# A gated cross-attention layer with a mixture of experts: the dispatch of tokens rewritten

## The chip, the core and the metric

The kernel runs on one core of one Trainium2 chip. The core has TensorE (matmuls; PE in the profile, its weight loads PEld), VectorE (DVE), ScalarE (ACT), GpSimd (POOL) and SyncE (SP), each with a queue of instructions that it works off in order. SyncE, ScalarE and GpSimd also start transfers (DMAs), which run on 16 engines that all of them share. The metric is the time on the device in microseconds (us), lower being better; the median of several runs is compared.

## The reference

The layer has two halves. In the first, 4096 tokens `x` of 512 numbers, normalised, attend to 3202 context rows, and four feature groups of each token go through the weights `W_qv`; the result, times tanh of a gate, is added to `x`. The second half is a mixture of eight experts:

```python
xf = layernorm(x)
gates = softmax(xf @ w_router + b_router)
topv, topi = top_k(gates, 2)                     # two experts for each token
cap = int(1.25 * n / e)                          # 640 places for each expert
onehot = one_hot(topi.reshape(-1), e)
pos = cumsum(onehot, axis=0)[arange, e_flat] - 1 # the token's place with its expert
keep = pos < cap
buf = zeros(e, cap, d).at[e_flat, posc].add(where(keep, xf[tok], 0))
h = gelu(einsum('ecd,edf->ecf', buf, w1) + b1)
out = einsum('ecf,efd->ecd', h, w2) + b2
# each kept token gets its experts' rows back, weighted by its gates over their sum
x = x + tanh(g_ffn) * y
```

What matters here: the places are handed out in the order of the tokens, so they need a running count per expert; and no expert can start before every token has been put in its place.

## The kernel before, in words

The tokens lie in tiles of 128 (`NT` = 32 tiles). The kernel has three stages.

**Attention** (to about 1532 us of the profile) works in eight groups of four tiles. It leaves behind, in DRAM, the transposed normalised tokens (`qT_d`) and a partial result for each tile (`r_d`). It also fills the experts' buffer `buf_d` with empty rows.

**Dispatch** (1532 to about 1700 us, lines 835 to 1054) takes the tiles in steps: seven steps of four and two of two (`STEPS`, line 877). `tile_mm` (line 882) loads a tile's share of `qT_d` and its `r` (three buffers), does eight matmuls into a PSUM tile `x1p` (line 895), lets VectorE add `r` to give the new token row `x1` (line 899), which ScalarE's queue stores to `out` (line 902). The logits of the router come from the same PSUM tile (lines 906 and 910). VectorE takes mean and variance of `x1` (lines 912 and 913).

`norms` (line 916) is called once for a step. GpSimd makes the scale 1/sqrt(variance + eps) for its tiles (lines 919 and 920, one addition and one power); VectorE scales the logits (922, 923); ScalarE writes the normalised row into `xn` (line 928).

`route` (line 932) chooses the two experts: maximum, exponentials (952), a one-hot mask for each choice (970 to 973), the sum `mask` (977), and the running counts `base` (984). `slots` (line 985) is called later: TensorE turns `mask` and `base` into positions in PSUM (987 and 988, `pos`); VectorE picks each choice's position and gate (994 to 997), tests it against `CAP`, divides the gates by their sum, writes them beside the row, and makes the row number `sidx` (1016 to 1022).

`dispatch` (line 1027) sends every tile twice: GpSimd starts an indirect DMA (line 1030) that scatters its 128 rows, 516 numbers each, to the rows `sidx` of `buf_d`; a row number past the end is dropped. There are 64 such scatters.

The order is that of the loop at its end: tiles of step g, `norms` of g, then `slots` and the scatters of step g - 2, then `route` of g - 1. A scheduler keeps this order on each queue where the instructions depend on each other, and may move others. So the scatters of a step stand on GpSimd's queue between the scales of two steps, and the positions of a step stand on TensorE's queue after the four tiles of a later step.

**Experts** (from about 1700 us). `expert_in` loads five blocks of 128 rows from `buf_d` (line 1128, three buffers `xb`), for expert 0 with a wait on all scatters; TensorE transposes them (line 111). Rows for the next expert are loaded during the present one. The weights come in halves: `load_half(e, h)` (line 827) loads 2 MB of `w1` (line 829) and 2 MB of `w2` (line 831) into one of two buffers each. Halves (0, 0) and (0, 1) are loaded in the dispatch, behind the loads of `qT_d` number 3 and 6 (line 887).

Of the kernel before, what the change touches and what calls it, by code (L numbers as in the profile page):

```python
# [14 lines left out]
P = 128  # L15
# [5 lines left out]
def gated_layer(ctx, tc, x, x_t, ctxt, ctxt_t, g_xattn, g_ffn, w_sim, w_sim1, b_sim, W_qv, W_qv_t, b_qv, b_qv_c, w_router, b_router, w1, b1, w2, b2, out):  # L21
# [814 lines left out]
    with ExitStack() as s2:  # L836
# [34 lines left out]

        scatters = []
        xg = {}
        prev_base = None


        STEPS = [list(range(t, t + G)) for t in range(0, NT - G, G)]
        STEPS += [list(range(t, t + G // 2)) for t in range(NT - G, NT, G // 2)]
        step_of = {t: k for k, ts_ in enumerate(STEPS) for t in ts_}
        qTs = {}  # L880

        def tile_mm(t, mv, lg):
            g, i = divmod(t, 4)
            if g not in qTs:
                qTs[g] = sb.tile([P, DC, TG], F32, name=f"q2T{g}", tag="q2T")
                ld = nc.sync.dma_start(qTs[g], qT_d[g])
                if g in (3, 6):
                    with tc.issue_after(ld.ins):
                        load_half(0, g // 6)
            r = sb.tile([P, 2, BW], F32, name=f"r2_{t}", tag="r2")  # L890
            nc.sync.dma_start(r, r_d[t])
            ps = ps_mm.tile([P, 2, 512], F32, name=f"x1p{t}", tag="mm")
            for j in range(2):
                for c in range(DC):
                    nc.tensor.matmul(  # L895
                        ps[:, j, :B1], qTs[g][:, c, i * P : (i + 1) * P], W1[:, c, j, :], start=(c == 0), stop=(c == DC - 1)
                    )
            x1 = sb.tile([P, D], F32, name=f"x1_{t}", tag="x1", bufs=G + 2)
            nc.vector.scalar_tensor_tensor(
                x1.rearrange("p (j d) -> p j d", j=2), ps[:, :, :256], tgx, r[:, :, :256], ALU.mult, ALU.add  # L900
            )
            nc.scalar.dma_start(out[t * P : (t + 1) * P, :], x1)

            k = t - STEPS[step_of[t]][0]
            l_ = lg[:, k, :]
            nc.vector.scalar_tensor_tensor(
# [3 lines left out]
            nc.vector.scalar_tensor_tensor(l_, ps[:, 1, 256:B1], sd[:, t : t + 1], l_, ALU.mult, ALU.add)  # L910
            st = sm.tile([P, 6], F32, name=f"st{t}", tag="st")
            nc.vector.bn_stats(st, x1)
            nc.vector.bn_aggr(mv[:, k, :], st)
            return x1

        def norms(k, x1s, mv, lg):
            n = len(x1s)
            rstd = sm.tile([P, G], F32, name=f"rstd{k}", tag="rstd")[:, :n]
            nc.gpsimd.tensor_scalar(rstd, mv[:, :n, 1], EPS, None, ALU.add)
            nc.gpsimd.tensor_tensor(rstd, rstd, neghalf.to_broadcast([P, n]), ALU.pow)  # L920
            l_ = lg[:, :n, :]
            nc.vector.tensor_tensor(l_, l_, rstd.unsqueeze(2).to_broadcast([P, n, E]), ALU.mult)
            nc.vector.tensor_tensor(l_, l_, br.unsqueeze(1).to_broadcast([P, n, E]), ALU.add)
            nb = sm.tile([P, G], F32, name=f"nb{k}", tag="nb")[:, :n]
            nc.vector.scalar_tensor_tensor(nb, mv[:, :n, 0], -1.0, rstd, ALU.mult, ALU.mult)
            xg[k] = sb.tile([P, G, R], F32, name=f"xn{k}", tag="xn", bufs=6)
            for i, x1 in enumerate(x1s):
                nc.scalar.activation(
                    xg[k][:, i, :D], x1, AF.Identity, scale=rstd[:, i : i + 1], bias=nb[:, i : i + 1]
                )  # L930

        def route(g, lg, prev):

            t0, n = STEPS[g][0], len(STEPS[g])

            def T(name, shape, dt=F32):
                a = sm.tile([G if k == "n" else G + 1 if k == "n+1" else k for k in shape], dt, name=f"{name}{g}", tag=name, bufs=3)
                return a[tuple(slice(0, n) if k == "n" else slice(0, n + 1) if k == "n+1" else slice(None) for k in shape)]

            def wide(a):  # L940
                return a.unsqueeze(2).to_broadcast([P, n, E])

            tt, ts, red = nc.vector.tensor_tensor, nc.vector.tensor_scalar, nc.vector.tensor_reduce
            revw = rev.unsqueeze(1).to_broadcast([P, n, E])
            mx = T("mx", [P, "n"])
            red(mx, lg, AX.X, ALU.max)
            d = T("d", [P, "n", E])
            tt(d, lg, wide(mx), ALU.subtract)

            ts(d, d, EXP_FLOOR, None, ALU.max)  # L950
            gate = T("gate", [P, "n", E])
            nc.scalar.activation(gate, d, AF.Exp)
            gs = T("gs", [P, "n"])
            red(gs, gate, AX.X, ALU.add)
            gi = T("gi", [P, "n"])
            nc.vector.reciprocal(gi, gs)
            tt(gate, gate, wide(gi), ALU.mult)


            oh = [T("oh0", [P, "n", E]), T("oh1", [P, "n", E])]  # L960
            rv = T("rv", [P, 2, "n"])
            eq = T("eq", [P, "n", E])
            left = T("left", [P, "n", E])
            for k in range(2):
                if k:
                    nc.vector.scalar_tensor_tensor(left, oh[0], -1000.0, d, ALU.mult, ALU.add)
                    red(mx, left, AX.X, ALU.max)
                    tt(eq, left, wide(mx), ALU.is_equal)
                else:
                    ts(eq, d, 0.0, None, ALU.is_equal)  # L970
                tt(eq, eq, revw, ALU.mult)
                red(rv[:, k, :], eq, AX.X, ALU.max)
                tt(oh[k], eq, wide(rv[:, k, :]), ALU.is_equal)


            mask = T("mask", [P, "n", E])
            tt(mask, oh[0], oh[1], ALU.add)
            base = T("base", [P, "n+1", E])
            if prev is None:
                nc.vector.memset(base[:, 0, :], 0.0)  # L980
            else:
                nc.vector.tensor_copy(base[:, 0, :], prev)
            for i in range(n):
                tt(base[:, i + 1, :], base[:, i, :], mask[:, i, :], ALU.add)
            def slots():
                ps = ps_po.tile([P, G, E], F32, name=f"pos{g}", tag="pos")[:, :n, :]
                nc.tensor.matmul(ps, upper, mask, start=True, stop=False)
                nc.tensor.matmul(ps, ones, base[:, :n, :], start=False, stop=True)

                pos = T("pos", [P, 2, "n"])  # L990
                gv = T("gv", [P, 2, "n"])
                tmp = T("tmp", [P, "n", E])
                for k in range(2):
                    tt(tmp, ps, oh[k], ALU.mult)
                    red(pos[:, k, :], tmp, AX.X, ALU.add)
                    tt(tmp, gate, oh[k], ALU.mult)
                    red(gv[:, k, :], tmp, AX.X, ALU.add)
                keep = T("keep", [P, 2, "n"])
                ts(keep, pos, float(CAP), None, ALU.is_lt)
                tt(gv, gv, keep, ALU.mult)  # L1000


                wsum = T("wsum", [P, "n"])
                tt(wsum, gv[:, 0, :], gv[:, 1, :], ALU.add)
                ts(wsum, wsum, 1e-6, None, ALU.max)
                nc.vector.reciprocal(wsum, wsum)
                ts(wsum, wsum, tgf, None, ALU.mult)  # L1007
                tt(
                    xg[g][:, :n, D : D + 2].rearrange("p g k -> p k g"),
                    gv, wsum.unsqueeze(1).to_broadcast([P, 2, n]), ALU.mult,  # L1010
                )
                nc.vector.tensor_copy(xg[g][:, :n, D + 2], tok[:, t0 : t0 + n])


                slot = T("slot", [P, 2, "n"])
                ts(slot, rv, -float(CAP), float(E * CAP), ALU.mult, ALU.add)
                tt(slot, slot, pos, ALU.add)
                ts(slot, slot, past, None, ALU.subtract)
                tt(slot, slot, keep, ALU.mult)
                sidx = T("sidx", [P, 2, "n"], I32)  # L1020
                ts(sidx, slot, past, None, ALU.add)
                nc.vector.tensor_copy(xg[g][:, :n, D + 3], sidx[:, 0, :])
                return sidx

            return base[:, n, :], slots

        def dispatch(g, sidx):
            for i in range(len(STEPS[g])):
                for k in range(2):
                    sc = nc.gpsimd.indirect_dma_start(  # L1030
                        out=buf_d[:, :],
                        out_offset=bass.IndirectOffsetOnAxis(ap=sidx[:, k, i : i + 1], axis=0),
                        in_=xg[g][:, i, :],
                        in_offset=None,
# [10 lines left out]
        for g in range(len(STEPS) + 1):  # L1045
# [4 lines left out]
            if half_routed is not None:  # L1050
                dispatch(g - 2, half_routed())
# [281 lines left out]
```

## Time and profile before

| What | Value |
|---|---|
| Median of 3 runs | 2716.5 us (2714.0 to 2717.52) |
| Profiled execution: its own time | 2714.11 us |
| Profiled execution: span, first to last instruction | 2712.3 us |
| TensorE busy in the span | 2642.9 us (97%) |
| VectorE busy | 1689.3 us (62%) |
| ScalarE busy | 419.8 us (15%) |
| GpSimd busy | 233.2 us (9%) |
| Mean granted TensorE clock | 0.984 of full speed |
| Dispatch: first and last matmul of a tile start | 1532.6 and 1657.8 us |
| Dispatch: first and last scatter start | 1583.6 and 1696.3 us |
| Experts: first transposition on TensorE | 1701.5 us |

The span is the time between the first and the last instruction of the one execution that the profiler recorded; the execution's own time lies 1.8 us above it. Times within the trace are counted from the span's start. A group of instructions is named by its line, engine, operation and tiles (written, then read). An engine's idle time is put down to what released it: `<-DVE mask L977` means that VectorE's instruction of line 977 came last of what was waited for; `issue` is time in which the profile shows nothing waited for. A matmul's end is modelled, so a busy TensorE is not a TensorE at its peak; the granted clock says how fast it was allowed to run.

### The profile page before, as it was taken

To read this page: it belongs to the slowest core of one execution; us is meant where nothing else is said; L and a number is where in the kernel's file an instruction comes from. 1 tells how busy PE (TensorE), PEld (TensorE's weight loads), DVE (VectorE), ACT (ScalarE), POOL (GpSimd) and SP (SyncE) were. 2 spreads that over 40 slices of the span, in tenths; PEclk is the share of its full clock that TensorE was granted. 3 is DMA by queue.
4 is the path that set the end of the run, shared out by engine and by line. 5 is a ranking of instruction groups with operands and counts; after the bars stand their busy time and mean duration, and the time that the engine had idled before them with its cause. 6 is when DMAs were issued, how large, how long until landed. Compare 5 with 4: busy or idle time off the path is not lost. (4 is left out here: it accounts for less than half of the span.)

```text
span 2712.3 us, 29984 instructions
## 1 busy us (share of the span) xinstructions
PE 2642.9 (97%) x11384; PEld 2130.5 (79%) x11384; DVE 1689.3 (62%) x3412; ACT 419.8 (15%) x673; POOL 233.2 (9%) x289
## 2 busy tenths in 40 slices
PE   8999999999999999999999994899999999999999
PEld 7648888888888888888888883677777777777776
DVE  7855755946837658459366576565747475655654
ACT  1200200201202102002011011111111111111111
POOL 0110000000001000000000036101001010101010
PEclk9898999999999999999999997899999999999999
DMA  7984765646746657467445794222323132322210
GB/s 260 270 296 174 190 208 155 226 159 175 229 154 173 230 154 227 155 181 234 147 145 187 241 362 142 90 86 94 112 105 118 68 124 86 132 82 105 82 59 20
DMA packets 184051, 436.65 MB, mean 161 GB/s; under 512 B 18616, under 2 KB 85165, under 8 KB 181858
## 3 DMA queue, kind: packets, MB, share of 16 engines
q1 hardware_dynamic: 157538, 357.48, 40.8%
q0 software_dynamic: 16624, 47.37, 5.3%
q10 hardware_dynamic: 9744, 29.87, 3.0%
q8 instruction: 90, 1.47, 0.2%
q14 instruction: 55, 0.45, 0.1%
HBM read 356.22 MB, written 85.60 MB: 163 GB/s over the span
## 5 line engine op out<-in xcount | busy, mean ns | idle before, releaser
L453 PE MATMUL pas<-Qp,kt 128*128 128x256 f32 (+1 forms) x728 | 175.5, 383 | 0.0
L1095 PE MATMUL pah<-bT,w 128*128 128x320 f32 x512 | 161.0, 437 | 0.8 <-DVE bT L1136 0.8
L570 PE MATMUL pbv<-E,vt 128*128 128x256 f32 (+1 forms) x728 | 159.5, 379 | 0.0
L570 PEld LDWEIGHTS pbv<-E,vt 128*128 128x128 f32 (+1 forms) x728 | 138.2, 190 | 18.9
L453 PEld LDWEIGHTS pas<-Qp,kt 128*128 128x128 f32 (+1 forms) x728 | 136.0, 188 | 21.4
L511 ACT ACTIVATE E<-E 128x1024 f32<-128x1024 f32 (+1 forms) x112 | 111.4, 996 | 156.5 <-DVE E L510 154.1
L510 DVE TENSOR_TENSOR E<-E,mb 128x1024 f32<-128x1024 f32 (+1 forms) x112 | 125.2, 1142 | 12.4 <-ACT mb L495 12.4
L1095 PEld LDWEIGHTS pah<-bT,w 128*128 128x128 f32 x512 | 98.0, 192 | 39.9 <-DVE bT L1136 1.2
L895 PE MATMUL x1p<-W,q2T 128*128 128x264 f32 x512 | 118.0, 391 | 3.3 <-DVE wsum L1007 1.6
L1095 PE MATMUL pao<-w,h 128*128 128x256 f32 x512 | 121.0, 379 | 0.0
L1270 POOL DMA_INDIRECT out<-acc,ti x40 | 42.8, 1070 | 859.4 <-DVE acc L1269 859.4
L895 PEld LDWEIGHTS x1p<-W,q2T 128*128 128x128 f32 x512 | 97.7, 192 | 21.2 <-PE x1p L895 3.6
L1247 PE MATMUL op<-w,h 128*128 128x512 f32 x256 | 113.7, 592 | 0.0
L471 DVE TENSOR_TENSOR M<-M,E 128x1024 f32<-128x1024 f32 (+1 forms) x96 | 109.0, 1136 | 6.7 <-ACT p1s L410 0.5
L1095 PEld LDWEIGHTS pao<-w,h 128*128 128x128 f32 x512 | 96.7, 190 | 16.7 <-issue 4.3
L410 ACT COPY p1s<-pas 128x512 f32<-128x512 f32 (+1 forms) x56 | 31.1, 554 | 499.0 <-issue 256.6
L426 DVE TENSOR_TENSOR E<-p4s,u3s 128x512 f32<-128x512 f32 (+1 forms) x56 | 36.5, 652 | 109.8 <-PE p4s L453 109.8
L522 DVE TENSOR_TENSOR SM<-SM,E 128x1024 f32<-128x1024 f32 (+1 forms) x80 | 89.1, 1114 | 0.0
L1247 PEld LDWEIGHTS op<-w,h 128*128 128x128 f32 x256 | 47.2, 190 | 52.0 <-issue 46.4
L453 PE MATMUL p6s<-q,kt 128*128 128x256 f32 (+1 forms) x364 | 87.2, 381 | 0.0
L453 PE MATMUL pbs<-q,kt 128*128 128x256 f32 (+1 forms) x364 | 86.6, 379 | 0.0
L453 PE MATMUL pbs<-Qp,kt 128*128 128x256 f32 (+1 forms) x364 | 86.6, 379 | 0.0
(411 smaller groups left out, 5247.2 us busy)
## 6 DMA issues: line engine op xcount, KB each, us to landing
kt<-kt_d SPq DMA_DIRECT2D x84, 896.0 KB
w<-in_w SPq DMA_DIRECT2D x32, 2048.0 KB
wp<-wt_d SPq DMA_DIRECT2D x56, 520.0 KB
vt<-vs_d SPq DMA_DIRECT2D x28, 896.0 KB
vt<-vs_d SPq DMA_DIRECT2D x28, 640.0 KB
kt_d<-ktb ACTq DMA_DIRECT2D x12, 896.0 KB
buf_d<-zero SPq DMA_DIRECT2D x80, 129.0 KB
xb<-buf_d SPq DMA_DIRECT2D x40, 258.0 KB
```

The costliest lines, as they stand in the source:

```text
L410: nc.scalar.copy(p1, cut(pa))
L426: tt(done(1, 0), cut(p4), u3, ALU.add)
L453: nc.tensor.matmul(ps[:w, jl, :], kts[j][:, KSLOT[p], k, :], B[p][:, k, :], start=start and jl == 0 and k == 0, stop=stop and k == 1, skip ...
L471: tt(m, m, e[:w, :, h], ALU.max)
L510: live[g]["last"] = tt(e, e, m, ALU.subtract)
L511: live[g]["exp"] = nc.scalar.activation(e, e, AF.Exp)
L522: tt(s, E_t[0][:, lr] if jj == 1 else s, e, ALU.add)
L570: mm = nc.tensor.matmul(ps[b], vt[: WJ[j], j - i * JH, b * P : (b + 1) * P], right(j), start=start and j == 0 and (b == 0 or g == 0), stop ...
L895: nc.tensor.matmul(ps[:, j, :B1], qTs[g][:, c, i * P : (i + 1) * P], W1[:, c, j, :], start=(c == 0), stop=(c == DC - 1))
L1095: nc.tensor.matmul(ps, a, b, start=start and i == 0, stop=stop and i == len(A) - 1, skip_group_check=True)
L1247: nc.tensor.matmul(ps, hT[:, k, 2 * MH :], W2[:, k, :], start=(k == 0), stop=(k == KH - 1))
L1270: sc = nc.gpsimd.indirect_dma_start(out=out[:, :], out_offset=rows_of(ti, s), in_=acc[:, :], in_offset=None, bounds_check=N - 1, oob_is_er ...
```

## The change

Only the dispatch and the place of one weight load change.

* The steps are six of four tiles and four of two.
* The sum of `x1` comes out of the addition that makes it; ScalarE squares `D*x1 - sum` and sums the squares (`ssd`), in place of VectorE's two statistics instructions. GpSimd makes the scale from `ssd`.
* `route` becomes `choose`, `slots` becomes `place`. The running count begins at each expert's first row (`first_i`), so that the position is the row number at once. The first gate is 1 over the sum of exponentials and the second `g2` over it, so gates are no longer looked up by mask. Two copies into `xn` go to ScalarE.
* The loop: `choose` of the step before, two tiles, `place` of the step before, scatters of two of its tiles, then (in steps of four) two more tiles; the step's scale; scatters of two more tiles. In steps of two, the scale comes before `place`, and one group of scatters follows.
* `r` has six buffers, `xn` five.
* `load_half(0, 1)` follows expert 0's row loads on SyncE's queue.

The diff, cut to its core:

```diff
-        STEPS = [list(range(t, t + G)) for t in range(0, NT - G, G)]
-        STEPS += [list(range(t, t + G // 2)) for t in range(NT - G, NT, G // 2)]
+        STEPS = [list(range(t, t + G)) for t in range(0, NT - 2 * G, G)]
+        STEPS += [list(range(t, t + G // 2)) for t in range(NT - 2 * G, NT, G // 2)]
...
-                if g in (3, 6):
+                if g == 3:
                     with tc.issue_after(ld.ins):
-                        load_half(0, g // 6)
-            r = sb.tile([P, 2, BW], F32, name=f"r2_{t}", tag="r2")
+                        load_half(0, 0)
+            r = sb.tile([P, 2, BW], F32, name=f"r2_{t}", tag="r2", bufs=6)
...
+            stt(
+                x1.rearrange("p (j d) -> p j d", j=2), ps[:, :, :256], tgx, r[:, :, :256], ALU.mult, ALU.add,
+                accum_out=s.sum[:, i : i + 1],
             )
             nc.scalar.dma_start(out[t * P : (t + 1) * P, :], x1)
+            junk = sb.tile([P, D], F32, name=f"jx{t}", tag="jx", bufs=2)
+            nc.scalar.activation(
+                junk, x1, AF.Square, scale=-float(D), bias=s.sum[:, i : i + 1], accum_out=s.ssd[:, i : i + 1]
+            )
...
-            nc.vector.bn_stats(st, x1)
-            nc.vector.bn_aggr(mv[:, k, :], st)
...
+        def scale(s):
+            s.rstd = small(f"rstd{g}", [P, n])
+            nc.gpsimd.tensor_scalar(s.rstd, s.ssd, float(D) ** -3, EPS, ALU.mult, ALU.add)
+            return nc.gpsimd.tensor_tensor(s.rstd, s.rstd, neghalf.to_broadcast([P, n]), ALU.pow)
...
+            ps = ps_po.tile([P, G, E], F32, name=f"pos{g}", tag="pos")[:, :n, :]
+            nc.tensor.matmul(ps, upper, s.mask, start=True, stop=False)
+            nc.tensor.matmul(ps, ones, s.base, start=False, stop=True)
+            for k in range(2):
+                tt(tmp[:, k], ps, s.oh[:, k], ALU.mult)
+            red(pos, tmp, AX.X, ALU.add)
+            stt(keep, s.rv, float(CAP), pos, ALU.mult, ALU.add)
+            ts(keep, keep, float((E + 1) * CAP), None, ALU.is_lt)
+            stt(pos, pos, past, keep, ALU.subtract, ALU.mult)
+            ts(s.sidx, pos, past, None, ALU.add)
...
-        for g in range(len(STEPS) + 1):
-            if g < len(STEPS):
-                norms(g, [tile_mm(t, mv, lgs[g]) for t in STEPS[g]], mv, lgs[g])
-            if half_routed is not None:
-                dispatch(g - 2, half_routed())
-            if g >= 1:
-                prev_base, half_routed = route(g - 1, lgs[g - 1][:, : len(STEPS[g - 1]), :], prev_base)
-        dispatch(len(STEPS) - 1, half_routed())
+        for g in range(len(STEPS)):
+            if prev is not None:
+                choose(prev)
+            for i in range(2):
+                mm = tile_mm(s, i)
+            if s.n > 2:
+                with tc.issue_after(mm.ins):
+                    place_prev()
+                send(2)
+                for i in range(2, s.n):
+                    tile_mm(s, i)
+            sc = scale(s)
+            if s.n == 2:
+                with tc.issue_after(mm.ins):
+                    place_prev()
+            with tc.issue_after(sc.ins):
+                send(2)
+            prev, s = s, s.next
+        choose(prev)
+        place_prev()
+        send(NT)
...
         nxt = expert_in(0)
+        with tc.issue_after(row_loads[-1]):
+            load_half(0, 1)
```

`send(n)` pops up to n tiles off the list of routed ones and scatters each twice; `issue_after` keeps what it holds behind the named instruction on its queue.

## The prediction

> **What bounds the kernel now.** I read the slices of the page first: TensorE is at 9 tenths nearly everywhere, with one deep dip (4) in the 25th slice, where POOL has its only crowded ones (3, 6, 1). So the place is the dispatch, 1532 to 1700 us. Then a table by stretches (columns: length, then busy time and count of PE, weight loads, DVE, ACT, POOL, then granted clock, DMA share, GB/s):
>
> ```profile
> 1532.30:1546.80 14.50, 14.50 (x67) 12.36 (x67) 6.12 (x19) 0.00 (x0) 0.00 (x0) 1.00 0.80 282
> 1546.80:1561.00 14.20, 14.20 (x65) 12.15 (x64) 10.43 (x47) 3.05 (x5) 1.30 (x2) 1.00 0.92 348
> ...
> 1604.70:1621.70 17.00, 15.10 (x69) 12.39 (x68) 8.56 (x52) 3.05 (x5) 7.16 (x9) 1.00 1.05 411
> ...
> 1658.10:1697.30 39.20, 2.55 (x13) 2.22 (x11) 19.05 (x125) 3.24 (x6) 30.05 (x33) 0.57 0.16 52
> 1697.30:1713.50 16.20, 9.72 (x32) 6.63 (x32) 10.02 (x31) 2.14 (x3) 7.92 (x10) 0.57 0.68 213
> ```
>
> While tiles are projected TensorE sets the pace: 14.24 us per four tiles, 3.56 each. Once the last tile is done at 1658.1, it idles for 39.2 us, POOL busy for 30.05 of them. The waits say on whom:
>
> ```profile
> SPq L1128 <- DMA buf_d<-xn,sidx: 47.0, 3, 38.5
> ...
> PE bps L111 <- DMA xb<-buf_d: 20.2, 2, 19.9
> ...
> DVE lg L922 <- POOL rstd L920: 24.6, 9, 4.9
> DVE x L899 <- DMA r<-r_d: 7.1, 2, 6.0
> ```
>
> SyncE holds expert 0's first row load until the last scatter has landed; VectorE in turn waits nine times for POOL's scale; two tiles came late from DRAM. POOL's timeline shows why scatters run late:
>
> ```profile
> 1583.56 1.15 POOL L1030 DMA_INDIRECT buf_d<-xn,sidx  x1 [4.96 <-DVE left L966]
> 1585.01 1.00 POOL L1030 DMA_INDIRECT buf_d<-xn,sidx  x1 [0.30 <-issue]
> ...
> 1661.71 0.97 POOL L1030 DMA_INDIRECT buf_d<-xn,sidx  x1 [0.30 <-issue]
> 1662.71 0.26 POOL L919 TENSOR_SCALAR rstd<-mv 128x2 f32<-128x2 f32 x1
> 1663.05 0.72 POOL L920 TENSOR_TENSOR rstd<-rstd,neghalf 128x2 f32<-128x2 f32 x1
> ...
> 1696.28 0.97 POOL L1030 DMA_INDIRECT buf_d<-xn,sidx  x1 [0.30 <-issue]
> ```
>
> The first of 64 scatters starts 51 us into the stage; from 1652.6 POOL is solid, one every 1.275 us (0.97 busy, 0.30 to issue), the scale queued behind eight. So 27 still stand at 1658.1. After 1697.3 the expert's start is a fixed sequence.
>
> **The change, part by part.**
>
> *The POOL queue.* A step's scatters went out after the projection two steps later; now they start in the middle of the next one. As the changed kernel's instructions stand on POOL, each scale has four scatters before and four behind it; behind the very last scale stand twelve. Total POOL work is 64 x 1.275 + 10 scales x 1.36 (L919 0.24, gap 0.08, L920 1.04) = 95 us, from about 1559: it has slack except at the end. Not 27 but 12 then follow the last tile: 15 x 1.275 = 19.1 us less.
>
> *Variance by squares.* Removed from VectorE per tile: L912 0.685 and L913 0.18. Added: an accumulator to the x1 sum and a Square on ScalarE, with the store's issue in front of it on ScalarE's queue. Prices by the nearest rows:
>
> ```profile
> L705 DVE SCALAR_TENSOR_TENSOR jz<-qT,ebb x32: 687/700/705, 154.1 to 1464.2; 128x512 f32<-128x512 f32 x32
> L705 DVE DVE_READ_ACCUMULATOR jz<-qT,ebb x32: 85/98/104, 154.7 to 1464.8; 128x1 f32 x32
> ...
> L702 ACT ACTIVATION_READ_ACCUMULATOR ebb<-ebb x8: 185/186/187, 132.3 to 1448.1; 128x1 f32 x8
> ...
> L902 ACTq DMA_DIRECT2D out<-x x32: 338/372/377, 1537.1 to 1666.8; - x32
> ```
>
> From the start of a step's last x1 sum to its scale: sum 0.75 + 0.10, store issue 0.37, Square 0.90 (0.80 of L928, with the 0.19 reading partly overlapped; between 0.62 of L702's plain form and 0.99), POOL 1.36, four handovers 0.25: **3.73 us** (3.41 for two tiles, L920 being 0.72). Before: 1546.99 to 1550.20 = 3.21. A loss of 0.5, on the path. Bounds 3.2 to 4.0.
>
> A rule speaks against this: "ScalarE: Activation LUTs", table sets, says functions come in sets, names exp, tanh, relu, abs for the exp set but not Square, and a change of set costs about 2.7 us. By it, Square and Exp alternating would cost two loads in each of ten steps, 54 us on ScalarE, perhaps half on the path: slower than before. The trace has a load at 1.28 (L1207), so 26 us. But the changed kernel's instructions hold the same two loads as before, ahead of Tanh and of Gelu: I take nothing.
>
> *Shorter routing, and the new wait.* VectorE loses about 14 small instructions a step (gate normalisation, gv products, slot arithmetic), each 0.15 to 0.2, half of that in pitch. They overlapped waits, so I credit only the chain. What matters is where the position matmuls now stand: after the **second** tile of the next step, not after the fourth. They need that step's bases. From the scale, by the pitches of the first step in the trace (0.22 between dependent instructions, 0.11 otherwise): six to eq +1.17, the next x1 sum 0.11 + 0.77, then rv to mask +4.15, three base sums, done +4.77. Before the position matmul, then: 0.2 + 3.73 + 4.77 = 8.7 us after the step's start; two tiles take 7.12. TensorE waits in order, the next tile behind it, resuming at 8.9: **1.8 us per step** (0.36 of it the pair itself, which before had too). Against it go the late r rows and the mid-step stalls of before. Bounds: 0.36 (chain in time) to 3.
>
> First step 1532.5 + 14.24; five of 16.0 give 1626.8. In the four steps of two, the sum of a step's second tile follows the base sums on VectorE, so a loop forms: 3.41 + (six and the sum, 1.9; rv to bases, 2.35) = 7.65, over TensorE's 7.48. With 8.8 for the first, the last sum starts at 1626.8 + 8.8 + 3 x 7.65 = 1658.6, the last tile having ended at 1658.1, **as before**. POOL does not stand in that loop: four scatters and a scale are 6.1 of 7.65; in the steps of four, scatters end at about 17.3 where the scale is wanted at 18.4, a margin of 1.1.
>
> *End.* Last sum 1658.6 + 3.41 = 1662.0; twelve scatters 15.3, less the last gap 0.3: 1677.0. The last step's choice and place (about 7.5 us) lie beside the first eight, 10.2 us. Before 1697.25: **20.2 us gained**.
>
> *load_half(0, 1)* goes behind expert 0's row loads: 4.2 MB, 10.4 us at the 405 GB/s of the crowded stretch. It takes them out of 1591 to 1625, where DVE waited 7.1 us for r. Passed on SyncE are expert 1's rows: they follow it in the ring, landing about 21 us after expert 0's first row load is issued (6.0 to its last, 10.4 for the weights, 2.6 for the 1.06 MB of gathers, 2 their own), where VectorE's row arithmetic asks for them at about 24.7 (1723.3 less 1698.6). Cover 3 us; without it up to 4 us late. The weights themselves are asked for at 1739 before, 40 us after: free. Six r buffers instead of three, tok and index copies on ScalarE (0.2 each): hidden, ScalarE has over 6 us free of 16. The iota and `first_i` run before the stage: nothing.
>
> *DMA.* Scatters move 24 us earlier, onto w(0,0). From 1547 to 1600: w 4.2, q2T 3.7, r 3.5, stores 3.5, scatters about 5.1 MB = 20 MB in 53 us, 377 GB/s against 405. It just fits; r is six deep. Zero to 7 us.
>
> Profiled execution: span 2712.3, 2714.1 with what lies around it, 2.4 under the median 2716.5 of the three runs shown. 2714.1 - 20.2 = 2693.9; from the median 2696.3. I say **2696**.
>
> **The rivals.**
> 1. *Bases in time.* The trace's first steps of before ran at 14.2 without stall, but with the matmul at the step's end. If the chain fits, TensorE needs 114 + 9 x 0.36 and ends near 1650: 28 us, 2688.
> 2. *Crowded DMA.* r waits of 7.1 us seen when weights met scatters. Against: half those weights are gone from there, and prefetch doubles. 13 us gained, 2703.
> 3. *No change.* The order is as the change says, so the scale does leave the eight scatters; what could eat the gain is expert 0: rows of expert 1 or weights late by much more than my 4. For it: one queue behind 4 MB. Against: DMA stood at zero GB/s after 1716. 2714 to 2716.
> 4. *Slower: scatters lengthen.* "GPSIMD Engine Reference", specifications, says POOL's memory interface is shared with VectorE, contended by its two-input instructions; moved between them, scatters could take longer. Row: 967/972/1836 ns min, median, max, with VectorE 11.6 of 16 us busy beside them; by the row nothing. With pitch d the cost is 5 x (4(d - 1.275) - 1.1) + 4 x (4d + 1.1 - 7.65) + 12(d - 1.275): it decides from d = 1.93. At a doubled 2.55: 20 + 15 + 15 = 50 us, net 30 slower, 2746.
>
> **How the numbers follow.** Forecast 0.56, rival 1 0.15, rival 2 0.16, no change 0.05, slower 0.08. Within 0.2% (5.4 us) is what this measurement can't tell from nothing. Faster 0.87, same 0.05, slower 0.08. Range: down to rival 1 and a little (2686), up past rival 2 with late expert rows (2706); what lies beyond is 13%.
>
> **What would show it.** First scatter near 1559; at most four between scales; 12 after the last one; last scatter about 19 us behind the last tile, not 39; the position matmul waiting on mask or base for 1 to 2 us in nearly every step; r waits gone; no further table load. Wrong if POOL's pitch leaves 1.28, if the last tile ends beyond 1665, or if expert 0 waits for rows of expert 1.

## The result, and the profile after

| | Before | Changed |
|---|---|---|
| Median on the same chip, 4 runs each | 2716.1 us (2714.0 to 2717.5) | 2695.7 us (2692.9 to 2699.3) |
| Profiled execution: own time, span | 2714.1, 2712.3 us | 2696.2, 2694.4 us |
| First tile's first matmul | 1532.55 us | 1533.07 us |
| Last scatter over (POOL's next work) | 1697.22 us | 1677.54 us |
| Between the two | 164.7 us | 144.5 us |

The ratio of the times is 0.9926 (95% interval 0.9909 to 0.9943): faster by 0.57 to 0.91%. In the profiled pair 20.2 us are gained between the first tile and the last scatter. The span is only 17.9 us shorter: the attention ended 0.5 us later in the changed kernel's profile, and 1.8 us are lost again when the first expert starts.

By stretches of the changed kernel (columns as before: length, busy time and count of PE, weight loads, DVE, ACT, POOL, then clock, DMA share, GB/s):

```profile
1563.00:1583.00 20.00, 19.20 (x88) 16.07 (x87) 11.13 (x56) 7.50 (x18) 12.14 (x15) 1.00 1.04 409
...
1658.10:1677.60 19.50, 1.42 (x8) 1.21 (x7) 10.90 (x50) 3.03 (x8) 14.37 (x16) 0.56 0.09 25
1677.60:1693.60 16.00, 9.11 (x28) 6.10 (x28) 9.93 (x31) 2.15 (x3) 7.70 (x10) 0.57 0.76 251
```

The stretch between last tile and last scatter has shrunk from 39.2 to 19.5 us; the next one, the start of expert 0, is nearly as long as it was (16.0 us for 16.2). GpSimd works early (12.14 us of work from 1563 to 1583, where before it did 2.52 from 1561 to 1583), and the DMAs are full there: 409 GB/s. The waits answer to those shown of before; the last-scatter wait of SyncE is 26.8 instead of 38.5 us at most, and VectorE waits for r no more:

```profile
SPq L1170 <- DMA buf_d<-xn,sidx: 35.4, 3, 26.8
...
PE bps L111 <- DMA xb<-buf_d: 16.2, 1, 16.2
```

TensorE's timeline in the middle of the stage (start, length, instruction, and in brackets the idle time before it):

```profile
1571.00 0.41 PE L1014 MATMUL pos<-mask,upper 128*128 128x32 f32 x2 [0.61 <-issue]
...
1571.85 14.49 PE L912 MATMUL x1p<-W,q2T 128*128 128x264 f32 x64
1586.93 0.41 PE L1014 MATMUL pos<-mask,upper 128*128 128x32 f32 x2 [0.60 <-DVE rv L981]
```

From position matmul to position matmul 15.93 us, of which 14.24 are tiles. In every step of four TensorE waits 0.6 us for the mask, and 0.19 for the base; the rest are the two small matmuls themselves. The brackets name another instruction or none, but VectorE's timeline has the mask ready just before the matmul starts:

```profile
1586.69 0.19 DVE L996 TENSOR_TENSOR mask<-oh 128x32 f32<-128x32 f32 x1
```

The last Square of the same step (ScalarE), GpSimd around its scale, and GpSimd at the end:

```profile
1581.10 0.19 ACT L923 ACTIVATION_READ_ACCUMULATOR jx<-x,sum 128x1 f32 x1
```

```profile
1579.66 0.98 POOL L1045 DMA_INDIRECT buf_d<-xn,sidx  x1 [0.30 <-issue]
1581.37 0.19 POOL L939 TENSOR_SCALAR rstd<-ssd 128x4 f32<-128x4 f32 x1 [0.73 <-issue]
```

```profile
1660.51 0.72 POOL L940 TENSOR_TENSOR rstd<-rstd,neghalf 128x2 f32<-128x2 f32 x1
1661.43 1.06 POOL L1045 DMA_INDIRECT buf_d<-xn,sidx  x1 [0.19 <-DVE keep L1033]
...
1676.58 0.98 POOL L1045 DMA_INDIRECT buf_d<-xn,sidx  x1 [0.30 <-issue]
```

The scale starts 0.08 us after the Square's sum is read out (1581.29), and 0.73 us after the four scatters in front of it: that gap is the margin between two ways round a loop. **Way A**: scale, choice on VectorE, position matmul, two more tiles, last sum, Square, scale. **Way B**: scale, choice, position matmul, placing on VectorE, four scatters, scale. Here B ends 0.73 us earlier than A, in the last two steps of four 0.58. After the last scale stand twelve scatters.

### The profile page after: what moved, and what is told of

It is laid out like the page before. It is cut to its first block, busy times and chain, and to the rows that moved or that the text cites. A ratio compares the mean times of both kernels' runs of the same rounds, so it can differ in the third digit from the quotient of the medians.

```text
span 2694.4 us, 29935 instructions
## 1 busy us (share of the span) xinstructions
PE 2644.3 (98%) x11388; PEld 2130.5 (79%) x11388; DVE 1671.4 (62%) x3283; ACT 449.6 (17%) x768; POOL 241.0 (9%) x292
## 5 line engine op out<-in xcount | busy, mean ns | idle before, releaser
L912 PEld LDWEIGHTS x1p<-W,q2T 128*128 128x128 f32 x512 | 96.7, 190 | 16.1
```

Of the source, the lines that this page charges most:

```text
L912: mm = nc.tensor.matmul(ps[:, j, :B1], qTs[g][:, c, q * P : (q + 1) * P], W1[:, c, j, :], start=(c == 0), stop=(c == DC - 1))
```

## The experiments

The length between first tile and last scatter is compared, read from each trace as in the table above, because the attention in front of it ends at 1531 to 1535 us from run to run. It comes from one trace for each run; two traces of the changed kernel agree to 0.01 us. The times of e2, e3, e4, e5, e11 and e12 are not clearly told apart from the changed kernel's, so that for these the length alone speaks. "Step" is from one position matmul (in the order of before: one scale) to the next in steps of four.

| Run | Length, us | Step, us | Time, us |
|---|---|---|---|
| Before | 164.7 | about 16.5 | 2716.1 |
| Changed | 144.5 | 15.93 | 2695.7 |
| e1 order undone | 155.5 | 14.69 | 2707.9 (2706.5 to 2710.1) |
| e2 place at step's end | 146.2 | 14.69 | 2696.9 (2695.0 to 2699.0) |
| e3 place after third tile | 149.8 | 16.1 to 16.3 | 2699.7 (2697.8 to 2701.5) |
| e4 weights back | 147.6 | 15.93, last 17.59 | 2698.0 (2697.5 to 2699.3) |
| e5 last eight 4, 2, 2 | 145.2 | 15.93 | 2696.3 (2694.7 to 2699.1) |
| e6 statistics on VectorE | 155.8 | 17.2 | 2708.5 (2706.9 to 2710.5) |
| e7 before, r and weights | 161.6 | 16.4 | 2713.7 (2710.3 to 2716.7) |
| e8 late, then mid | 150.8 | disturbed | 2704.6 (2701.9 to 2705.1) |
| e9 before, squares alone | 158.4 | uneven | 2709.7 (2707.9 to 2711.8) |
| e10 long routing | 153.1 | 16.8 to 17.1 | 2705.0 (2701.6 to 2709.3) |
| e11 Square before store | 144.0 | 15.51 | 2695.6 (2693.0 to 2698.1) |
| e12 changed again | 144.5 | 15.93 | 2697.5 (2694.1 to 2699.0) |

**e1: only the order put back.**

```diff
-            if prev is not None:
-                choose(prev)
-            for i in range(2):
-                mm = tile_mm(s, i)
...
+            for i in range(s.n):
+                tile_mm(s, i)
+            scale(s)
+            norm(s)
+            if g >= 2:
+                place_held()
+            if prev is not None:
+                choose(prev)
+                held.append(prev)
```

`norm` scales the logits and writes `xn`; `place_held` places the step two before and sends its eight scatters. `xn` gets six buffers again, for five.

> The changed kernel with only the old order put back: a step's scale and normalisation first, then the position matmul and all eight scatters of the step two before, then the choice for the step one before. Squares on ScalarE, the shorter routing, six r buffers, the late second half of the weights and the last eight tiles by twos all stay. Theory (the gain is the order on POOL's queue): the gain goes nearly all, last scatter between 1690 and 1700 us, time 2708 to 2716 us. Rival (the gain comes from the other parts: shorter routing, r rows in time, twos): last scatter stays below 1682, time 2700 us or less.

Neither number came: 155.5 us, 11.0 more than changed, 9.2 less than before. The tiles run at 14.69 us per four without a stall until the steps of two, where the scales stand behind eight scatters, 12.7 us apart, and TensorE waits (GpSimd's timeline, then TensorE's):

```profile
1646.51 0.19 POOL L939 TENSOR_SCALAR rstd<-ssd 128x2 f32<-128x2 f32 x1
...
1659.16 0.19 POOL L939 TENSOR_SCALAR rstd<-ssd 128x2 f32<-128x2 f32 x1
```

```profile
1650.12 6.69 PE L912 MATMUL x1p<-W,q2T 128*128 128x264 f32 x16 [4.74 <-DVE oh L990]
...
1665.79 0.61 PE L1018 MATMUL pos<-mask,upper 128*128 128x16 f32 x2 [8.63 <-DVE tmp L1023]
```

So the order is worth 11 us beside the other parts, not all 20. What gives the rest was the question from here on.

**e2: position matmul at the step's end, eight scatters behind the scale.**

```diff
-            for i in range(2):
+            for i in range(s.n):
                 mm = tile_mm(s, i)
...
             sc = scale(s)
-            if s.n == 2:
-                with tc.issue_after(mm.ins):
-                    place_prev()
+            with tc.issue_after(mm.ins):
+                place_prev()
             with tc.issue_after(sc.ins):
-                send(2)
+                send(4)
```

> The position matmul stands behind a step's last tile instead of its second, and all its scatters behind the scale. Theory (the position matmul in mid-step costs TensorE 1.3 us in each of five steps, and the last scatter follows the last tile): steps of four take 14.6 us instead of 15.9, their end 6.7 us earlier; eight scatters at once stand before the second scale of the steps of two, which gives back some 3.7; eight instead of twelve scatters behind the last scale. Last scatter near 1671, time 2689 us. Rival (POOL's total, not TensorE, sets the end): scatters start one half step later and the end stays at 1677 or moves later, time 2696 to 2700 us.

The stall is gone as the theory says (14.69), but the gain is more than given back. I had counted one lot of eight scatters in front of a scale of the steps of two; there are two:

```profile
1635.79 0.97 POOL L1045 DMA_INDIRECT buf_d<-xn,sidx  x1 [0.30 <-issue]
1636.84 0.19 POOL L939 TENSOR_SCALAR rstd<-ssd 128x2 f32<-128x2 f32 x1
...
1649.50 0.19 POOL L939 TENSOR_SCALAR rstd<-ssd 128x2 f32<-128x2 f32 x1
```

In length 1.7 us are lost. Both scales follow the scatters with no idle time shown, 12.7 us apart where the loop of two takes 7.57. GpSimd's queue takes back what TensorE wins.

**e3: position matmul behind the third tile.**

```diff
-            for i in range(2):
+            for i in range(min(3, s.n)):
                 mm = tile_mm(s, i)
...
-                for i in range(2, s.n):
+                for i in range(3, s.n):
```

> The position matmul stands behind the third tile of a step of four instead of the second; nothing else is changed. Theory (bases are there 8.7 us after a step's start, three tiles take 10.7): the stall is gone, steps of four take 14.6 us instead of 15.9, all behind them comes 6.7 us earlier, last scatter near 1671, time 2689 us. Rival (the scatters, 1.8 us later in each step, now stand before the scale and push it, so that the chain of scale and choice stretches the steps again): no gain, 2694 to 2698 us.

The rival's mechanism: the scatters start later and push the scale, which has lost its gap, and TensorE waits for the mask all the same.

```profile
1581.35 0.97 POOL L1045 DMA_INDIRECT buf_d<-xn,sidx  x1 [0.30 <-issue]
1582.39 0.19 POOL L939 TENSOR_SCALAR rstd<-ssd 128x4 f32<-128x4 f32 x1
```

```profile
1587.73 0.41 PE L1014 MATMUL pos<-mask,upper 128*128 128x32 f32 x2 [0.77 <-DVE mask L996]
```

Here way B decides. The length grew by 5.3, more than the rival had. By the distances between scales, 2.1 of these come where the first scatters hold the second scale, 1.0 in the four turns after it (16.1 to 16.3 us for 15.9), and the rest in the steps of two, one of which takes 10.03 us for 7.56.

**e4: second half of the weights back in the dispatch.**

```diff
-                if g == 3:
+                if g in (3, 6):
                     with tc.issue_after(ld.ins):
-                        load_half(0, 0)
+                        load_half(0, g // 6)
...
-        with tc.issue_after(row_loads[-1]):
-            load_half(0, 1)
```

> The second half of expert 0's weights is loaded inside the dispatch again, as before the change, with six r buffers and everything else as changed. Theory 1 (the late load keeps expert 1's rows out, so four transposes no longer fill TensorE's wait before expert 0's second product, it idles 1.85 us instead of 1.09, and the granted clock falls to 0.5 for 4 us): the transposes are back in the gap, the clock stays at 1.0 from then on, first full-clock product about 2 us nearer to the first row, time 2693.5 us. Theory 2 (the load was moved because r rows came late): r waits of 3 to 7 us return in the dispatch, time 2697 to 2703 us.

Both in part. The transposes are back, and the clock stays up after them. But the stage is 3.1 us longer. DMAs run at 408 and 410 GB/s from 1606 to 1635, where the changed kernel has 312 and 260. VectorE has its `r` in time; what comes late is the store of x1 on ScalarE's queue, 2.5 us after its sum began instead of 0.8, with the Square behind it. SyncE's timeline, then ScalarE's:

```profile
1604.63 0.38 SPq L831 DMA_DIRECT2D w<-in_w  x1
1615.31 1.64 SPq L908 DMA_DIRECT2D r<-r_d  x3
```

```profile
1629.10 0.34 ACTq L920 DMA_DIRECT2D out<-x  x1
1629.48 0.72 ACT L923 ACTIVATE jx<-x,sum 128x512 f32<-128x512 f32 x1 [4.43 <-DMA r<-r_d]
```

The bracket names a load of `r`, and rightly. By the trace's semaphore record this store reports its landing on the same semaphore as the `r` load of a tile two further on (issued at 1615.73, the second of the three above, behind the weights), and its queue waits until that load has reported in full, at 1629.02. So `r` is late, as theory 2 has it, but a store pays for it.

That step takes 17.59 us, 1.7 more. The other 1.4 us of the 3.1 follow from it: TensorE waited 2.25 us, its clock fell (0.89 in the mean of the next 15 us), and 32 matmuls took 8.74 instead of 7.37 us.

**e5: last eight tiles as 4, 2, 2.**

```diff
-        STEPS = [list(range(t, t + G)) for t in range(0, NT - 2 * G, G)]
-        STEPS += [list(range(t, t + G // 2)) for t in range(NT - 2 * G, NT, G // 2)]
+        STEPS = [list(range(t, t + G)) for t in range(0, NT - G, G)]
+        STEPS += [list(range(t, t + G // 2)) for t in range(NT - G, NT, G // 2)]
```

> The changed kernel with the last eight tiles in steps of 4, 2 and 2, as before the change; all else as changed. With the order undone the last scatter came at 1687 instead of 1697, so about 10 of the 20 us come from other parts. Theory 1 (the steps of two are not among them: a step of four takes 15.9 us and two of two 15.1, and twelve scatters follow the last scale either way): 1 us later, time 2696 to 2697 us. Theory 2 (the smaller last steps bring most of the other ten): last scatter at 1682 or later, time 2701 to 2705 us.

0.7 us longer: the twos are worth about that, since twelve scatters stand behind the last scale either way.

**e6: statistics on VectorE again.**

```diff
-                accum_out=s.sum[:, i : i + 1],
-            nc.scalar.activation(
-                junk, x1, AF.Square, scale=-float(D), bias=s.sum[:, i : i + 1], accum_out=s.ssd[:, i : i + 1]
-            )
+            nc.vector.bn_stats(st, x1)
+            nc.vector.bn_aggr(s.mv[:, i, :], st)
```

> The changed kernel with mean and variance by VectorE's statistics as before, no Square on ScalarE and no accumulator on the x1 sum. Theory 1 (VectorE's 0.87 us per tile come back into the choice, which stands between scale and position matmul): a step of four takes 17 us instead of 15.9, last scatter 6 us later, time 2701 us. Theory 2 (the squares only lengthen the way from the last sum to the scale, 3.47 us against 3.21): a step of four takes 15.7 us, time 2694 us.

Theory 1, and larger than I had it: 11.3 us longer. GpSimd and TensorE:

```profile
1581.99 0.97 POOL L1043 DMA_INDIRECT buf_d<-xn,sidx  x1 [0.30 <-issue]
1582.99 0.26 POOL L937 TENSOR_SCALAR rstd<-mv 128x4 f32<-128x4 f32 x1
```

```profile
1606.15 0.41 PE L1012 MATMUL pos<-mask,upper 128*128 128x32 f32 x2 [1.79 <-DVE st L929]
...
1623.35 0.41 PE L1012 MATMUL pos<-mask,upper 128*128 128x32 f32 x2 [1.87 <-DVE oh L980]
```

The scale's gap is gone, and TensorE waits 1.8 instead of 0.6. Choice (4.6 instead of 4.2 us from scaled logits to mask) and placing both have tiles' statistics between their instructions; B becomes the longer way. From the first to the sixth position matmul 86.15 us instead of 79.58; the three steps of two after it 27.9 instead of 23.2.

**e7: before, with six r buffers and the late weights alone.**

```diff
-                if g in (3, 6):
+                if g == 3:
                     with tc.issue_after(ld.ins):
-                        load_half(0, g // 6)
-            r = sb.tile([P, 2, BW], F32, name=f"r2_{t}", tag="r2")
+                        load_half(0, 0)
+            r = sb.tile([P, 2, BW], F32, name=f"r2_{t}", tag="r2", bufs=6)
...
+        with tc.issue_after(row_loads[-1]):
+            load_half(0, 1)
```

> The kernel before, with two parts of the change alone: six r buffers instead of three, and the second half of expert 0's weights behind its row loads. Theory 1 (VectorE's waits for r rows are on the path that sets the end): r waits gone, last scatter 5 to 7 us earlier, time 2708 to 2711 us. Theory 2 (POOL's queue sets the end, the tiles may come sooner or later): last scatter within 2 us of 1697, time 2713 to 2717 us.

Between the two: r waits gone, 3.1 us shorter, 2713.7 us; its ratio to before is 0.9993 (0.9986 to 1.0). In time that is at the edge of what is told apart. The scales stay 16.4 us apart behind eight scatters.

**e8: e2's order in steps 1 to 4, the changed order from step 5 on.**

```diff
-            for i in range(2):
+            late = s.n > 2 and g < 5
+            for i in range(s.n if late else 2):
                 mm = tile_mm(s, i)
-            if s.n > 2:
+            if s.n > 2 and not late:
...
-                send(2)
+                send(4 if late else 2)
```

> The changed kernel with the position matmul at the step's end and all eight scatters behind the scale in steps 1 to 4 alone; step 5 and the steps of two as changed. Theory (with the matmul at the end a step took 14.69 us instead of 15.93; what gave the gain back in the run with this order everywhere was two lots of eight scatters in front of the scales of the first two steps of two): four steps at 14.7, 5 us gained there; step 5 loses up to 1 as four scatters still stand before its mid-step lot; last scatter near 1673.5, time 2691 to 2692 us. Rival (POOL is the bound from there on, and takes it back): last scatter 1676 to 1678, time 2695 to 2696 us.

Longer by 6.3, by neither theory: VectorE waited 4.4, 6.0 and 3.8 us before the last sum of three steps, for something that the trace only calls remote, where e2 with the same code in these steps waited 2.4 for the matmuls. The trace's semaphore record says a little more: each of the three sums starts just after a signal of TensorE (1580.57, 1597.10 and 1611.41), and these signals come 2.0, 3.8 and 3.5 us after the modelled end of the tile's last matmul. Why they came late isn't settled, and so the run says nothing about the order.

**e9: before, with the squares alone.**

```diff
+                accum_out=mv[:, k, 0:1],
...
+            nc.scalar.activation(
+                junk, x1, AF.Square, scale=-float(D), bias=mv[:, k, 0:1], accum_out=mv[:, k, 1:2]
+            )
...
-            nc.vector.bn_stats(st, x1)
-            nc.vector.bn_aggr(mv[:, k, :], st)
```

> The kernel before with one part of the change alone: the variance by ScalarE's squares with the mean from an accumulator on the x1 sum, no statistics on VectorE. With the statistics put back into the changed kernel a step of four grew from 15.93 to 17.2 us. Theory 1 (VectorE's work between a scale and the next scatter is on the loop in the old order too: POOL waits 5.1 us there in each step): that wait falls to about 4.2 us in some six steps, last scatter 4 to 7 us earlier, time 2709 to 2712 us. Theory 2 (the squares bring something only beside the new order): within 2 us of before, 2714 to 2717 us.

Theory 1: 6.3 us shorter, 2709.7 us; the ratio to before is 0.9979 (0.9969 to 0.9988).

**e10: changed, with the long routing.** The core of it; the sum of gates, the test against `CAP` and VectorE's two copies are as in the code before too.

```diff
+            nc.vector.reciprocal(gi, gs)
+            tt(gate, gate, wide(gi), ALU.mult)
...
+                tt(tmp, s.gate, s.oh[:, k], ALU.mult)
+                red(gv[:, k, :], tmp, AX.X, ALU.add)
...
+            ts(slot, s.rv, -float(CAP), float(E * CAP), ALU.mult, ALU.add)
+            tt(slot, slot, pos, ALU.add)
```

> The changed kernel with the routing arithmetic of before, all on VectorE: gates normalised, their products with the two one-hots, slots worked out from value and position, token and index copied by VectorE, 14 small instructions more in a step. Theory 1 (whatever VectorE does between a scale, the position matmul and the next scatter is on the loop): mask 0.3 us later, first scatter 1.3 us later, which pushes the next scale; a step of four takes 16.5 to 17 us, last scatter 5 to 8 us later, time 2701 to 2704 us. Theory 2 (they fall into VectorE's waits, so they were removed for nothing): a step of four stays within 0.2 us of 15.93, time 2696 to 2697 us.

Theory 1, 8.6 us longer: step 16.8 to 17.1, scale directly behind its scatters as in e3 and e6 (GpSimd's timeline):

```profile
1601.34 0.98 POOL L1053 DMA_INDIRECT buf_d<-xn,sidx  x1 [0.30 <-issue]
1602.39 0.19 POOL L939 TENSOR_SCALAR rstd<-ssd 128x4 f32<-128x4 f32 x1
```

**e11: Square issued before the store.**

```diff
-            nc.scalar.dma_start(out[t * P : (t + 1) * P, :], x1)
             nc.scalar.activation(
                 junk, x1, AF.Square, scale=-float(D), bias=s.sum[:, i : i + 1], accum_out=s.ssd[:, i : i + 1]
             )
+            nc.scalar.dma_start(out[t * P : (t + 1) * P, :], x1)
```

> The changed kernel with two lines of ScalarE exchanged: a tile's Square is issued before the store of its x1 instead of behind it. Theory (the store's issue, 0.37 us, stands on the loop from the last sum to the scale): sum to scale 3.1 us instead of 3.47, a step of four 15.56 instead of 15.93, last scatter 2 us earlier, time 2693.5 us. Rival (the step is set by the scale behind its four scatters, so that the Square may come sooner without effect): step within 0.1 us of 15.93, time 2695 to 2696 us.

In the steps of four as the theory has it, 15.51 us (TensorE waits 0.16 for the mask instead of 0.6). But the length is only 0.5 us shorter. In the steps of two VectorE's order came out differently (its timeline):

```profile
1644.28 0.16 DVE L1023 SCALAR_TENSOR_TENSOR keep<-rv,pos 128x4 f32<-128x4 f32 x1
1646.81 0.18 DVE L953 TENSOR_TENSOR lg<-lg,rstd 128x16 f32<-128x16 f32 x1 [2.37 <-POOL rstd L940]
1646.90 0.16 DVE L1024 TENSOR_SCALAR keep<-keep 128x4 f32<-128x4 f32 x1
```

An instruction that waits for the scale now stands in the middle of the placing, which the next scatters need. That step takes 8.6 us, and the last scale comes 8.65 us behind the one before it, where the changed kernel has 7.58. 2695.6 us beside 2697.5 of the changed kernel on that chip: not told apart. No run here beats the changed kernel by more than can be measured.

**e12: the changed kernel again.**

> The changed kernel itself once more beside the others. All theories: 2694 to 2697 us, a step of four 15.93 us. Whether the granted clock falls to 0.5 again for 3.4 us after expert 0's first transposes, as in its first trace, is open: if it is tied to the order of instructions it falls again, if it is tied to the moment it may not, and the first full-clock product then follows the first transpose about 1.7 us sooner.

144.5 us and 15.93, as in the first trace. The clock fell again (below).

## Why the prediction came true, step by step

| Step of the sum | Predicted | Measured |
|---|---|---|
| First scatter | near 1559 | 1559.95 |
| Last sum to scale, steps of four | 3.73 | 3.47 |
| Step of four | 16.0 | 15.93 |
| Margin of the scatters before the scale, steps of four | 1.1 | 0.73 to 0.58 |
| Loop of two | 7.65 | 7.57 |
| Last tile's end | 1658.1 | 1658.1 |
| Last scale over | 1662.0 | 1661.2 |
| Last scatter over | 1677.0 | 1677.5 |
| Scatters behind the last scale | 12 | 12 |
| Given back later | 0 | 1.8 |

The length fits to 0.1 us. That the median of the times (2695.7) lies 0.3 us from the forecast is in part luck: the medians of before and changed are 20.4 us apart, the profiled executions 17.9, and the start of the dispatch alone differs by 4.6 us between the traces.

*POOL's queue.* Order and counts are as forecast, and the pitch stayed at 1.275 us, so the rival of lengthening scatters fell. What failed is what the step credits: "15 x 1.275 = 19.1 us less" was booked on the order of the queue. Undoing the order alone costs 11.0 us. The 19.1 is a right difference between two states, but the order is only one cause of it.

*Variance by squares.* "A loss of 0.5, on the path" has the wrong sign. The way from last sum to scale is indeed 0.26 longer (3.47 for 3.21; the Square took 0.72, the store's issue 0.38). But e6 shows 11.3 us lost without the squares and e9 6.3 us gained by them in the old order. I counted them between sum and scale only; what counts is that VectorE's 0.87 us per tile leave the choice and the placing, which lie on both ways of the loop. The rule of the table sets, which the prediction weighed and put at nothing, made no difference: the only table load in the trace between 1500 and 1760 us is that of expert 0 (1691.86, 1.28 us), as before.

*Shorter routing.* "They overlapped waits, so I credit only the chain": wrong as well, it is worth 8.6 us (e10). That VectorE has idle time in a step (busy 9.8 of 16 us from 1571 to 1587) says nothing of the stretch between scale and scatter: from the first scaled logits (1582.72) to the row's gates (1591.00) its timeline shows no idle time.

The sum came out right all the same because its chain for the changed kernel (4.77 us to the bases, 3.73 to the scale) was counted from the changed kernel's own instructions, with squares and short routing already in it. It was the account of the causes that failed, not the time.

The parts do not add: order 11.0, squares 11.3, routing 8.6, weights 3.1, twos 0.7 is 34.7 us for a gain of 20.2. With ways A and B 0.73 us apart, the squares or the long routing alone make B the longer one, and then every step is longer (e6, e10); the order costs its 11.0 in the steps of two (e1). With two parts put back, the second would find some of the damage done. No run puts back two, so this last step is argued.

*The new wait.* 1.8 us per step forecast, 15.93 - 14.24 = 1.69 measured. That it could not simply be moved away (e2, e3) the prediction did not see. It had the margin of GpSimd's queue (1.1 us) but took it for slack, and TensorE's stall for a cost of its own; the two are sides of one loop.

*The other rivals.* Bases were not in time. The DMAs were crowded (409 GB/s), but r, six deep, was not late. *Rows of expert 1* did not hold expert 0: TensorE is busy 36.35 of 36.4 us from 1693.6 on. That the late weights were worth moving shows in e4, 3.1 us of length; e7 has another 3.1, but with six `r` buffers besides. In time neither is clear of noise.

*The 1.8 us given back*: 1.7 of them are a fall of the granted clock, in the next section.

## What the runs showed of the hardware

After expert 0's transposes the granted clock rose to 1.0, TensorE idled 1.85 us for VectorE, and the clock fell back to 0.5. The changed kernel, then e2, TensorE's timeline:

```profile
1693.64 1.45 PE L1135 MATMUL p6h<-x,w1s 128*128 128x320 f32 x4 [1.85 <-DVE x L1191]
1694.89 2.34 PE L1135 MATMUL p7h<-bT,w 128*128 128x320 f32 x4
1697.03 1.81 PE L1135 MATMUL pbh<-x,w1s 128*128 128x320 f32 x4
```

```profile
1696.05 1.34 PE L1128 MATMUL p6h<-x,w1s 128*128 128x320 f32 x4 [2.06 <-DVE x L1184]
1697.23 1.24 PE L1128 MATMUL p7h<-bT,w 128*128 128x320 f32 x4
```

Same matmuls: 2.34 us at half clock, 1.24 at full, and e2's wait was the longer. In all fourteen traces the clock rises there; in seven it falls again, each time 3.41 us after the rise, and is back after another 3.41, which costs half of that, 1.7 us. What differs is how much of the gap lies within the 3.41 us after the rise. These windows in the changed kernel and in e2 (TensorE's busy time is the second number):

```profile
1691.34:1694.75 3.41, 1.55 (x6) 0.87 (x5) 3.41 (x9) 1.81 (x2) 1.00 (x1) 1.00 1.02 410
```

```profile
1692.42:1695.84 3.42, 1.56 (x8) 0.84 (x7) 3.28 (x10) 1.77 (x2) 1.77 (x2) 1.00 1.01 392
```

In these windows TensorE was busy for 1.34 to 1.36 us (five traces), 1.50 and 1.55 where the clock fell, and for 1.51, 1.56, 1.67, 1.70, 1.78, 1.78 and 2.20 where it stayed. The whole traces say the same. Up to the end of the program, all changes of the clock within a trace lie on one grid of 3.41 us. Of the windows of that grid at full clock, from 300 us on in all fourteen traces, all 42 with less than 1.5 us of work were followed by half clock, none of the 9618 with more than 1.7 us, and three of the ten between. So here the clock fell by a test of activity in fixed windows with a limit between 1.5 and 1.7 us, and where a gap falls in the window decides; with modelled ends of matmuls the limit can't be read closer. (Near 100 and 203 us the clock falls at busier windows too; that is not explained.)

The Trainium skill ("TensorE: Matmul & The Clock Gate", Part 1) has the same window, free-running; its rule of no gaps above some 3.4 us ("HAM oscillation") is too lax by these traces, where gaps of 1.85 to 2.06 us were enough. Before, four transposes of expert 1 stood in the gap; the late weights moved them away (e4 has them back). In the three traces that have them there, the clock stayed, but so it did in four of eleven without them.

The second is e4's: a store whose semaphore still belonged to an earlier load was held for 1.7 us until that load had landed, and what is computed behind it on ScalarE waited too. DMAs at 410 GB/s alone don't do that: the changed kernel has 409 GB/s from 1563 to 1583, and there the store in front of a step's last Square comes 0.80 us after its sum began (1580.05).

## What to carry over

Before crediting an edit to the place where it stands, close the loop: list every way from one scale to the next, engine by engine, with its length, because an edit on the longest way counts in each turn and parts that share a way don't add. Work taken off an engine that idles more than a third of a step can still be worth some 10 us if it lay between a release and the next one. A stall that a loop puts on one engine is only worth moving if the other ways round have slack for it; here they had 0.73 us at most.
